# Cross-attention with text and prompt keys: when a Gram's rows are sent, and two moves in the first batch

## The chip, the cores and the metric

The kernel runs on one core of one Trainium2 chip. The metric is the device time of one execution in microseconds. The core has a matrix engine (TensorE; PE in the profile, with PEld for its weight loads), a vector engine (VectorE, DVE), an activation engine (ScalarE, ACT), a general engine (GpSimd, POOL), and SyncE (SP), which here issues nearly all DMAs. Each engine works through its own queue in order, and an instruction waits on semaphores for what it needs; whatever stands behind a waiting instruction on that engine waits too. An issue of a DMA takes time on SP's queue, and the data land later. Accumulators for matmuls lie in PSUM, in banks.

## The reference

Eight batches of 112 query rows with 320 channels attend, in 20 heads of 16 channels, to 375 context rows of 512 channels: 371 text rows and 4 prompt rows ("ip"). Besides the usual text attention, each head's attention-weighted mean of the raw context (`qsem`) is compared by cosine with the normalised prompt rows, and this similarity joins the prompts' logits.

```python
q, k_t, v_t = heads(hidden @ W_q), heads(text_ehs @ W_k), heads(text_ehs @ W_v)
probs_t = softmax(einsum("bhsd,bhtd->bhst", q, k_t) * Dh**-0.5)
text_out = einsum("bhst,bhtd->bhsd", probs_t, v_t)
k_ip, v_ip = heads(ip_ehs @ W_k_ip), heads(ip_ehs @ W_v_ip)
qsem = l2norm(einsum("bhst,bte->bhse", probs_t, text_ehs))
sem = einsum("bhse,bne->bhsn", qsem, l2norm(ip_ehs))
probs_ip = softmax(einsum("bhsd,bhnd->bhsn", q, k_ip) * Dh**-0.5 + 0.5 * sem)
ip_out = einsum("bhsn,bhnd->bhsd", probs_ip * spatial_mask, v_ip)
out = (text_out + ip_out) @ W_out + b_out + hidden
```

## The kernel before

The kernel never forms `qsem`. For each batch it makes the Gram matrix of the context rows (375 x 375, its upper triangle, `gram`, L516), beside it a column of ones and the values of one head. A head's probabilities, multiplied with this wide matrix `u`, give at once the product with the Gram (whose sum with the probabilities is the squared length of `qsem`), the products with the normalised prompts, the sum of the probabilities, and the text output. All in float32.

**Steps.** A step is a batch b and a group g of four heads, five groups to a batch, 40 steps. In a step TensorE does the big product of four heads (`multiplied`, L768, twelve blocks j = 0 to 11, each four matmuls, one for each head in its own 32 rows of the array and its own PSUM bank), and the scores of the step two ahead (`scores`, L709): the heads 2 and 3 at the step's start, the heads 0 and 1 at block j = 6. `probabilities` (L738) takes the maxima on DVE (`nmx`, L742), the exponentials on ACT (L745), and `sent` (L751) copies each head's probabilities by a DMA from SP into `xg` (L754), where the four heads lie as the transposition wants them. `xg` is a ring of two buffers: a step's buffer is that of the step two before. In the step before they are needed, at j = 2, DVE transposes them in blocks of 32 (`transposed`, L756, instruction L762) into `xgT`. After the product, ACT copies out the narrow columns (`value_sums`, L791) and DVE multiplies each bank with the probabilities and sums (`reduced`, L823, "junk"), which also frees the bank.

**Between products** TensorE computes the next batch's Gram (after g = 0), values (after g = 1 and 2) and keys (after g = 2, 3 and 4), projections of queries, and the rest of the batch before (`finish`, L844). The function `between` (L1112) writes this order out. `transposed_context` (L429) turns the context of a later batch for this, in three pieces on DVE (L437, for batches from 2 on); `run(("c", n), ...)` takes one piece.

**The wide matrix.** `doubled` (L502) writes the Gram into the tile `ug`, whose 128 partitions hold four blocks of 32 context rows. The product needs each block under every one of the four heads' 32 rows, so `gram_to_groups` (L549) copies each of four blocks (`QN`, numbered 0 to 3) four times (`parts`, one for each head's rows a) into `u`: sixteen DMAs from SP for a batch, 99 KB each (L553), each a whole row of `u` with the columns kept for the values. `u` has two buffers. The values go to DRAM (`values_to_dram`, L626) and come back by four DMAs as `vr` (`values_to_groups`, L632). Then `placed` (L681) copies, on GpSimd, the values of one group into the value columns of `u`, in three pieces (L688): for the next group of the same batch once the present product has read the old ones, and for g = 0 of the next batch at the end of step (b, 4), once all rows of its `u` and its `vr` have landed.

**What sets the order.** TensorE, SP, DVE and (in the main loop) ACT run the order in which the program issues; on GpSimd the framework chooses the order, except in the last batch. In the loop from L1246, a step issues the first pair's scores and probabilities, then the product with its insertions at j = 0, 2 and 6, then the second pair's probabilities, the sums, and behind them loads, `between` and the writing of the values. So SP sees in a step: the first pair's two sends; what is issued at j = 2; the second pair's two sends; what follows the second pair. The steps (6, 3) and (6, 4), ahead of the last batch, send three pairs instead of two: of those, the middle one (`more`) has its scores made at j = 0 and is sent at j = 2, ahead of the Gram's pieces there. In step (0, 3) (`late`) the first pair comes inside the product at j = 0. The last batch has a loop of its own (L1337).

In the first batch the prompts' projections are done by `prompt_projections` (L296), in pieces at the ends of (0, 1), (0, 2) and (0, 3); the second makes `kipb`, the prompts' keys under a mask, for `prompt_logits` (L690) at the end of (0, 4).

Of the kernel before, what the change touches and what calls it, by code (L numbers as in the profile page):

```python
# [20 lines left out]
def kernel(  # L21
# [14 lines left out]
    nc = tc.nc  # L36
# [259 lines left out]
    def prompt_projections():  # L296

        both = work.tile([2 * N, CP], F32, tag="ipkv", name="ipkv", bufs=1)
        kp = both[:N]
        last = kp[:, FULL * P :].rearrange("n (a r d) -> n a r d", r=2, d=D)  # L300
        nc.gpsimd.memset(last[:, :, 1, :], 0.0)
        ps = bank("ps_ipkv")
        for e in range(NE):
            for i, w in enumerate((wkip_sb, wvip_sb)):
                nc.tensor.matmul(
                    ps[i * N : (i + 1) * N, :C],
                    ipT[:, e, :],
                    w[:, e, :],
                    start=(e == 0),
                    stop=(e == NE - 1),  # L310
                )
        nc.scalar.copy(kp[:, : FULL * P], ps[:N, : FULL * P])
        nc.scalar.copy(
            last[:, :, 0, :], ps[:N, FULL * P : C].rearrange("n (a d) -> n a d", d=D)
        )
        nc.scalar.copy(both[N : 2 * N, :C], ps[N : 2 * N, :C])
        yield

        ps = bank("ps_kip")
        for i in range(NC):  # L320
            nc.tensor.transpose(
                ps[:, i * N : (i + 1) * N], kp[:, i * P : (i + 1) * P], ident[:N, :N]
            )
        nc.scalar.copy(kip, ps[:, : NC * N].rearrange("p (i n) -> p i n", n=N))
        for i in range(NC):
            nc.vector.tensor_tensor(
                kipb[:, i],
                kip[:, i, :NIP].unsqueeze(1).to_broadcast([P, HC, NIP]),
                hmask.unsqueeze(2).to_broadcast([P, HC, NIP]),
                ALU.mult,  # L330
            )
        yield

        nc.sync.dma_start(vipd, both[N : 2 * N, :C])
        yield
# [213 lines left out]
    def gram_to_groups(b, blocks, eng=nc.sync, parts=range(GROUP)):  # L549

        for q in blocks:
            for a in parts:
                eng.dma_start(  # L553
                    st[b]["u"][a * RG : (a + 1) * RG, q * GW : (q + 1) * GW],
                    ug[q * RG : (q + 1) * RG, :],
                )
# [181 lines left out]
    def probabilities(b, g, a, hold=False):  # L738
        s = st[b]
        ps = s.pop(("sc", g, a))  # L740
        nmx = small.tile([S, 1], F32, tag="nmx", name=f"nmx_{b}_{g}_{a}", bufs=4)
        nc.vector.tensor_reduce(nmx, ps[:S, :TT], AX.X, ALU.max, negate=True)  # L742
        if ("p", g) not in s:
            s["p", g] = home(b, g)
        nc.scalar.activation(s["p", g][:, a, :], ps[:S, :TT], AF.Exp, bias=nmx)  # L745
        if b > 0:
            nc.scalar.copy(s["ipl"][:, groups[g][a], :], ps[:S, TT:T])  # L747
        if not hold:
            sent(b, g, a)
# [355 lines left out]
    def run(key, make, pieces=1):  # L1105

        if key not in gens:
            gens[key] = make()
        for _ in range(pieces):
            next(gens[key], None)  # L1110

    def between(b, g):  # L1112

        nb = b + 1
        new = nb < B


        first = [bs for bs in pairs if bs[0] == (nb if b == 0 else nb + 1)]
        rest = [bs for bs in pairs if bs[0] == nb]
        if g == 0:  # L1120
            if new:
                run(("g", nb), lambda: gram(nb), 2)
            if new:
                run(("g", nb), None)
            if b == 0:
                run(("v", nb), None)
            if b > 0 and new:
                run(("f", b - 1), lambda: finish(b - 1))
        if g == 1:
            if new:  # L1130
                run(("v", nb), lambda: values(nb), 1 if b == 0 else 2)
            if b == 0:
                run(("pp",), prompt_projections)
        if g == 2 and new:
            run(("k", nb), lambda: keys(nb))
            run(("v", nb), None)
            for bs in first if b == 0 else ():
                run(("q", bs[0]), None)
        if g == 2 and b > 0 and new:
            run(("f", b - 1), None, 2)  # L1140
        if g == 3:
            if new:
                run(("k", nb), None, 1)
            if b > 0 and new:
                run(("f", b - 1), None)
            for bs in rest:
                run(("q", bs[0]), None)
        if nb + 1 < B and g in ((1, 2, 3) if b == 0 else (0, 1, 2)):
            run(("c", nb + 1), lambda: transposed_context(nb + 1))
        for bs in first:  # L1150
            if g in ((0, 1) if b == 0 else (2, 3)[: len(bs)]):
                run(("q", bs[0]), lambda: project_queries(bs))
        if g == 4:
            if b > 0 and new:
                run(("f", b - 1), None, 2)
            if nb < B - 1:
                run(("k", nb), None, 1)
            for bs in (first if b > 0 else []) + (rest if b < B - 2 else []):
                run(("q", bs[0]), None)
# [68 lines left out]
        (2, NG - 1): ((5, 0), (6, 1)),  # L1228
        (4, NG - 1): ((7, 0),),
    }  # L1230
    ctx_blocks = {1: (0,), 2: (1,), NG - 1: (2, 3)}
    halves = (range(GROUP // 2), range(GROUP // 2, GROUP))

    def ahead(n):

# [10 lines left out]
    for n, (b, g) in enumerate(steps[:-NG]):  # L1246
        now, more, then = ahead(n)
        late = (b, g) == (0, NG - 2)
        for c, a in now if not late else ():
            scores(*c, a)  # L1250
            probabilities(*c, a)
        for j, _ in enumerate(multiplied(b, g)):
            if j == 0:
                for c, a in now if late else ():
                    scores(*c, a)
                    probabilities(*c, a)
                for c, a in more:
                    scores(*c, a, ps=bank(f"ps_s_{c[0]}_{c[1]}_{a}"))
                    probabilities(*c, a, hold=True)
            if j == 6:  # L1260
                for c, a in then:
                    scores(*c, a)
            if j == 2:
                if g == 0:
                    gram_banks(b + 1)
                transposed(*steps[n + 1])
                for c, a in more:
                    sent(*c, a)
                if 1 <= g <= 3:
                    gram_to_groups(b + 1, {1: (0,), 2: (1,), 3: (3,)}[g], parts=halves[g == 2])  # L1270
                for c, i in x_loads.get((b, g), ())[: int(n > 0)]:
                    load_x_blocks(c, i)

                if g in (1, 2) and b > 0:
                    run(("f", b - 1), None)
        value_sums(b, g)
        if g == 2 and b > 0:
            run(("f", b - 1), None)
        if n == NG - 1:
            run(("t", b), lambda: prompt_logits(b))  # L1280
        for c, a in then:
            probabilities(*c, a)
        if n == len(steps) - NG - 1:
            sums = shared(b, g, GROUP // 2)
            next(sums)
            reduced(b, g, 2)
        else:
            reduced(b, g)
        placed(*steps[n + 1])
        if g == 0 and b > 1:  # L1290
            run(("f", b - 2), None)
        load_rest(n)
        if n == 0:
            load_next(2)
        if g in ctx_blocks and b < B - 3:
            load_ctx_blocks(b + 3, ctx_blocks[g])
        for c, i in x_loads.get((b, g), ())[1:]:
            load_x_blocks(c, i)
        if g == 1:
            gram_to_groups(b + 1, (0,), parts=halves[1])  # L1300
            gram_to_groups(b + 1, (1,), parts=halves[0])
        elif g == 2:
            gram_to_groups(b + 1, (2,))
        elif g == 3:
            gram_to_groups(b + 1, (3,), parts=halves[1])
            values_to_groups(b + 1)
        if g in (2, 3) and b == 0:
            run(("pp",), None)
        if (b, g) == (B - 2, 0):
            prompt_values_by_head()  # L1310
        if (b, g) == (B - 2, 1):
            bd = load_prompt_values_by_head()
        if g == 0 and b > 0:
            prompt_values(b - 1)
        between(b, g)
        if g == 1:
            values_to_dram(b + 1, nc.sync, 0, 2)
        if g == 2:
            values_to_dram(b + 1, nc.sync, 2)
# [137 lines left out]
```

## Time and profile before

| | us |
|---|---|
| median of 3 runs | 426.23 (425.27 to 430.86) |
| the profiled execution | 426.04 |
| its span in the profile | 424.3 |
| DMA: mean rate over the span | 155 GB/s |
| xg sends: count, each | 156, 162.3 KB |
| u pieces: count on SP, each | 124, 99.0 KB |

The profile was taken on one execution; its time of 426.04 us is the span of 424.3 and 1.7 us around it, and all positions below are microseconds from the start of the span. The granted clock was 0.999. A row of an engine's instructions in order of time has start, length, engine, line, operation, what is written and read, and their number; in brackets the idle time of the engine ahead of it and what ended it. A row of the busy time by stretches has the stretch, its length, then for PE, PEld, DVE, ACT and POOL the busy time with the number of instructions, the clock, and the DMA engines' share and rate.

### The profile page before, as it was taken

To read this page: it belongs to the slowest core of one execution; us is meant where nothing else is said; L and a number is where in the kernel's file an instruction comes from. 1 tells how busy PE (TensorE), PEld (TensorE's weight loads), DVE (VectorE), ACT (ScalarE), POOL (GpSimd) and SP (SyncE) were. 2 spreads that over 40 slices of the span, in tenths; PEclk is the share of its full clock that TensorE was granted. 3 is DMA by queue.
4 is the path that set the end of the run, shared out by engine and by line. 5 is a ranking of instruction groups with operands and counts; after the bars stand their busy time and mean duration, and the time that the engine had idled before them with its cause. 6 is when DMAs were issued, how large, how long until landed. Compare 5 with 4: busy or idle time off the path is not lost.

```text
span 424.3 us, 14021 instructions
## 1 busy us (share of the span) xinstructions
PE 415.8 (98%) x5500; PEld 327.3 (77%) x5500; DVE 331.5 (78%) x693; ACT 185.5 (44%) x647; POOL 111.2 (26%) x277
## 2 busy tenths in 40 slices
PE   8999999999998999999999999999999999999995
PEld 8867767878776977779778887788778887787993
DVE  5037668869896987889789987987898986888873
ACT  2344332335333463334533463333634363446773
POOL 6411100011160120602133220602124120515550
PEclk9999999999999999999999999999999999999999
DMA  8676846565766565666656556655555556465200
GB/s 256 184 191 198 187 122 181 155 174 152 192 157 169 141 170 154 158 175 175 169 142 167 144 158 164 159 145 158 167 151 151 134 162 181 135 167 166 66 2 29
DMA packets 61687, 65.84 MB, mean 155 GB/s; under 512 B 22072, under 2 KB 55648, under 8 KB 61622
## 3 DMA queue, kind: packets, MB, share of 16 engines
q1 hardware_dynamic: 60990, 63.98, 56.5%
q8 instruction: 44, 0.72, 0.8%
q10 hardware_dynamic: 632, 0.96, 0.7%
q14 instruction: 21, 0.17, 0.1%
HBM read 20.23 MB, written 5.32 MB: 60 GB/s over the span
## 4 chain that ended last, share of the span: by engine, by line
PE 83%; DVE 4%; ACT 3%; DMA 3%; issue 3%; SPq 2%; POOL 0%; DVEq 0%; POOLq 0%
PE ps_qd L781 34%; PE ps_v L611 14%; PE ps_k L577 10%; PE ps_s L719 9%; PE ps_g L535 7%; DMA xg<-p 2%; PE ps_q L377 2%; PE ps_o L995 2%; PE ps_g L491 1%; DVE xgT L762 1%; DVE nmx L742 1%; ACT shared L820 1%; SPq L553 1%; PE ps_w L467 1%; SPq L636 1%
## 5 line engine op out<-in xcount | busy, mean ns | idle before, releaser
L781 PE MATMUL ps_qd<-u,xgT 32*112 32x360 f32 (+11 forms) x3840 | 219.5, 351 | 1.2 <-POOL u L688 1.2
L781 PEld LDWEIGHTS ps_qd<-u,xgT 32*112 32x112 f32 x3840 | 189.1, 172 | 27.0 <-POOL u L688 2.4
L762 DVE STREAM_TRANSPOSE xgT<-xg 128x1536 f32<-128x1536 f32 (+1 forms) x45 | 119.7, 2680 | 13.9 <-DMA xg<-p 9.4
L745 ACT ACTIVATE p<-ps_s,nmx 112x371 f32<-112x371 f32 x156 | 84.9, 586 | 61.5 <-DVE nmx L742 49.3
L742 DVE TENSOR_REDUCE nmx<-ps_s 112x1 f32<-112x371 f32 x160 | 76.9, 526 | 28.3 <-PE ps_s L719 27.3
L827 DVE CUSTOM_DVE_ANT_0 junk<-ps_qd,p 112x371 f32<-112x371 f32 x146 | 79.2, 543 | 17.9 <-PE ps_qd L781 1.5
L719 PE MATMUL ps_s<-kT,qm 32*112 32x375 f32 (+1 forms) x320 | 66.7, 497 | 0.0
L688 POOL COPY u<-vr 128x64 f32<-128x64 f32 x120 | 25.7, 236 | 152.5 <-PE ps_qd L781 90.2
L611 PE MATMUL ps_v<-wv_sb,ctxT 128*128 128x384 f32 (+1 forms) x192 | 63.0, 477 | 0.0
L611 PEld LDWEIGHTS ps_v<-wv_sb,ctxT 128*128 128x128 f32 x192 | 35.7, 190 | 20.9
L794 ACT COPY pvs<-ps_qd 112x21 f32<-112x21 f32 x151 | 16.2, 189 | 74.8 <-PE ps_qd L781 74.5
L577 PE MATMUL ps_k<-ctxT,wk_sb 128*128 128x371 f32 x136 | 46.9, 488 | 0.2 <-DVE ctxT L458 0.2
L577 PEld LDWEIGHTS ps_k<-ctxT,wk_sb 128*128 128x128 f32 x136 | 24.4, 189 | 14.0 <-issue 0.5
L719 PEld LDWEIGHTS ps_s<-kT,qm 32*112 32x112 f32 x320 | 23.7, 170 | 12.6 <-issue 10.9
L535 PE MATMUL ps_g<-ctxT 128*32 128x375 f32 (+11 forms) x672 | 30.4, 333 | 0.0
L535 PEld LDWEIGHTS ps_g<-ctxT 128*32 128x32 f32 x672 | 27.7, 110 | 2.0
L618 ACT COPY vext<-ps_v 128x384 f32<-128x384 f32 (+1 forms) x24 | 11.2, 465 | 40.0 <-PE ps_v L611 39.5
L747 ACT COPY ipl<-ps_s 112x4 f32<-112x4 f32 x140 | 24.3, 174 | 0.0
L386 DVE TENSOR_SCALAR qm<-ps_q,emask 128x224 f32<-128x224 f32 (+1 forms) x25 | 9.0, 394 | 17.3 <-PE ps_q L377 17.2
L970 POOL TENSOR_TENSOR wv<-vip,w 112x1280 f32<-112x1280 f32 x6 | 14.8, 2464 | 27.7 <-DVE w L910 27.7
L437 DVE STREAM_TRANSPOSE ctxT<-ct 128x512 f32<-128x512 f32 x18 | 20.0, 1110 | 0.0
L508 POOL TENSOR_TENSOR ug<-ug,half 128x128 f32<-128x128 f32 (+1 forms) x24 | 10.4, 447 | 30.6 <-ACT ug L507 30.6
(174 smaller groups left out, 320.7 us busy)
## 6 DMA issues: line engine op xcount, KB each, us to landing
xg<-p SPq DMA_DIRECT2D x156, 162.3 KB
u<-ug SPq DMA_DIRECT2D x124, 99.0 KB
ct<-in_ctx_dram SPq DMA_DIRECT2D x24, 176.0 KB
vr<-vd SPq DMA_DIRECT2D x32, 120.0 KB
vip<-vipd SPq DMA_DIRECT2D x6, 560.0 KB
vd<-vext SPq DMA_DIRECT2D x7, 320.0 KB
vd<-vext SPq DMA_DIRECT2D x7, 160.0 KB
out_dram<-ob SPq DMA_DIRECT2D x8, 140.0 KB
```

Of the source, the lines that this page charges most:

```text
L437: nc.vector.transpose(ctxT[:, :, c * P : (c + 1) * P].rearrange("p e (j i) -> p j e i", i=RG), ct[:, some, :].rearrange("p j (k e) -> p j ...
L535: nc.tensor.matmul(ps[c][q * RG : (q + 1) * RG, j * RG - c * P : T - c * P], ctxT[:, e, j * RG : (j + 1) * RG], ctxT[:, e, j * RG : T], st ...
L577: nc.tensor.matmul(ps[:, :TT], wk_sb[:, e, i * P : (i + 1) * P], s["ctxT"][:, e, :TT], start=(e == 0), stop=(e == NE - 1),)
L611: nc.tensor.matmul(ps[:, :w], ctxT[:, e, c * P : (c + 1) * P], wv_sb[:, e, :w], start=(e == 0), stop=(e == NE - 1),)
L688: nc.gpsimd.tensor_copy(v, dealt(b, c, s["vr"][:, c * QN : (c + 1) * QN, g, :]))
L719: nc.tensor.matmul(ps[:S, :w], qm[a * RG : (a + 1) * RG, i, r, j * S : (j + 1) * S], s["kT"][a * RG : (a + 1) * RG, i, :w], start=True, st ...
L742: nc.vector.tensor_reduce(nmx, ps[:S, :TT], AX.X, ALU.max, negate=True)
L745: nc.scalar.activation(s["p", g][:, a, :], ps[:S, :TT], AF.Exp, bias=nmx)
L747: nc.scalar.copy(s["ipl"][:, groups[g][a], :], ps[:S, TT:T])
L762: nc.vector.transpose(xT[:, j : j + n].rearrange("p j (k q) -> p q j k", q=QN), xg[:, :, j * RG : (j + n) * RG].rearrange("p q (j k) -> p ...
L781: nc.tensor.matmul(banks[a][:S, j * RG : UW], xT[a * RG : (a + 1) * RG, j, :S], region(b, c)[a * RG : (a + 1) * RG, q, j * RG - c * P :], ...
L827: nc.vector.tensor_tensor_reduce(out=junk, in0=ps[:S, :TT], in1=s["p", g][:, a, :], scale=1.0, scalar=0.0, op0=ALU.mult, op1=ALU.add, accu ...
```

## The change

Three things are moved.

1. A Gram's sixteen pieces. Before: step (b, 1) sends half of block 0 at j = 2 and, after the second pair, the other half and half of block 1; (b, 2) sends the other half of block 1 at j = 2 and block 2 after the second pair; (b, 3) sends half of block 3 at j = 2 and the other half after the second pair, ahead of the values' four DMAs. After: the steps (b, 1) to (b, 4) send blocks 0 to 3, one whole block of four DMAs each, at j = 2; only the values' four DMAs stay behind the second pair of (b, 3).
2. The context's blocks. Before, step (b, 4) loads blocks 2 and 3 of context b + 3; after, only block 2, and block 3 is loaded at j = 2 of step (b + 1, 0).
3. First batch. `kipb`'s three products go from VectorE to GpSimd; the third piece of context 2's transposition goes from the end of (0, 3) to (0, 4), behind the first pair's probabilities.

```diff
-            nc.vector.tensor_tensor(
+            nc.gpsimd.tensor_tensor(
                 kipb[:, i],
...
-        if nb + 1 < B and g in ((1, 2, 3) if b == 0 else (0, 1, 2)):
+        if nb + 1 < B and g in ((1, 2) if b == 0 else (0, 1, 2)):
             run(("c", nb + 1), lambda: transposed_context(nb + 1))
...
-    ctx_blocks = {1: (0,), 2: (1,), NG - 1: (2, 3)}
-    halves = (range(GROUP // 2), range(GROUP // 2, GROUP))
+    ctx_blocks = {1: (0,), 2: (1,), NG - 1: (2,)}
...
             probabilities(*c, a)
+        if (b, g) == (0, NG - 1):
+            run(("c", LEAD), None)
         for j, _ in enumerate(multiplied(b, g)):
...
                 for c, a in more:
                     sent(*c, a)
-                if 1 <= g <= 3:
-                    gram_to_groups(b + 1, {1: (0,), 2: (1,), 3: (3,)}[g], parts=halves[g == 2])
+                if g > 0:
+                    gram_to_groups(b + 1, (g - 1,))
+                if g == 0 and 0 < b < B - 2:
+                    load_ctx_blocks(b + 2, (QN - 1,))
...
-        if g == 1:
-            gram_to_groups(b + 1, (0,), parts=halves[1])
-            gram_to_groups(b + 1, (1,), parts=halves[0])
-        elif g == 2:
-            gram_to_groups(b + 1, (2,))
-        elif g == 3:
-            gram_to_groups(b + 1, (3,), parts=halves[1])
+        if g == 3:
             values_to_groups(b + 1)
```

## The prediction

> **What bounds the kernel now.** I read the page first: busy time, then the chain of waits.
>
> ```profile
> PE 415.8 (98%) x5500; PEld 327.3 (77%) x5500; DVE 331.5 (78%) x693; ACT 185.5 (44%) x647; POOL 111.2 (26%) x277
> ...
> PE 83%; DVE 4%; ACT 3%; DMA 3%; issue 3%; SPq 2%; POOL 0%; DVEq 0%; POOLq 0%
> ```
>
> TensorE is busy almost throughout, so work taken off DVE, ACT, POOL or SP is worth only what TensorE now waits for. The busy time by stretches shows where it waits for nothing: batch 2's end to batch 3's start.
>
> ```profile
> 150.10:199.20 49.10, 49.10 (x686) 38.19 (x684) 41.60 (x83) 20.76 (x76) 12.36 (x29) 1.00 0.62 165
> ```
>
> No idle time in 49.10 us. The gaps are elsewhere; TensorE's instructions in order of time give three of them, two marked idle and one inside a step. (A step (b, g) is a batch and a group; it begins with the scores of L719.)
>
> ```profile
> 89.23 3.89 PE L781 MATMUL ps_qd<-u,xgT 32*112 32x392 f32 x54 [0.68 <-POOL u L688]
> ...
> 98.92 0.57 PE L719 MATMUL ps_s<-kT,qm 32*112 32x375 f32 x2
> ...
> 104.99 5.43 PE L611 MATMUL ps_v<-wv_sb,ctxT 128*128 128x384 f32 x16
> ...
> 137.88 0.54 PE L568 MATMUL ps_k<-ident,k 128*128 128x128 f32 x3 [1.33 <-ACT ipl L747]
> ```
>
> ```profile
> 180.05 0.57 PE L719 MATMUL ps_s<-kT,qm 32*112 32x375 f32 x2
> ...
> 188.68 0.57 PE L719 MATMUL ps_s<-kT,qm 32*112 32x375 f32 x2
> ...
> 194.04 4.34 PE L535 MATMUL ps_g<-ctxT 128*32 128x375 f32 x96
> ```
>
> A step's product takes 194.04 - 188.68 = 5.36 us when undisturbed; in (1, 1) it takes 104.99 - 98.92 = 6.07, so 0.7 is lost there. With 0.68 and 1.33 that makes 2.7 us that a better order could return. A gain of over 2% (8.5 us; 2% is about what a measurement of this kernel can tell from no change) has no room.
>
> **The new wait.** Block 3 of a Gram moves from step (b, 3) to (b, 4), behind that step's first pair. The copy at L688 (`placed`) writes value columns over those the rows just brought, so `placed(b + 1, 0)` must wait for all sixteen pieces, and TensorE's first product of batch b + 1 waits for it. What counts is when the last pieces land against that product's start. Prices, first in step (2, 4):
>
> ```profile
> 182.06 0.58 ACT L745 ACTIVATE p<-ps_s,nmx 112x371 f32<-112x371 f32 x1
> ...
> 186.29 0.62 ACT L745 ACTIVATE p<-ps_s,nmx 112x371 f32<-112x371 f32 x1
> ```
>
> ```profile
> 180.69 2.16 SPq L636 DMA_DIRECT2D vr<-vd  x4
> 182.95 1.85 SPq L754 DMA_DIRECT2D xg<-p  x2
> 184.85 1.88 SPq L127 DMA_DIRECT2D xr_sb<-in_x_dram  x4
> 186.83 1.74 SPq L754 DMA_DIRECT2D xg<-p  x2
> ...
> 207.57 2.51 SPq L553 DMA_DIRECT2D u<-ug  x4
> ```
>
> ```profile
> 185.52 0.59 POOL L688 COPY u<-vr 128x64 f32<-128x64 f32 x3 [8.22 <-DMA vr<-vd]
> ```
>
> The first pair's second exponential ends at 182.64. SP today sends the pair from 182.95, because the value rows (vr) keep it until 182.85; with two u pieces fewer ahead of them it is free earlier, the pair goes at about 182.1 and is out at 183.9 (today's start would make it 184.8). Four u pieces take 2.51: out at 186.4 (187.3). From the end of issuing to landing the trace has no row for u; the nearest is vr: 182.85 to 185.5 = 2.65 here, and 86.54 to 88.94 = 2.40 in the first batch (rows below). A u piece is smaller, so I take 2.4. Landed at 188.8, first of the three copies (0.59 / 3 = 0.2, with its waits 0.3) at 189.1, against a product due at 188.7: 0.4 to 0.5 late, 1.35 by today's start. I take 0.5 (0.4 to 1.35), and the same for (3, 4) and (4, 4), on the assumption that their steps have this length of 8.63. Step (5, 4) is shorter:
>
> ```profile
> 325.07 0.57 PE L719 MATMUL ps_s<-kT,qm 32*112 32x375 f32 x2
> ...
> 333.22 0.57 PE L719 MATMUL ps_s<-kT,qm 32*112 32x375 f32 x2
> ```
>
> 8.15 instead of 8.63, so 1.0 late (0.9 to 1.8). Together 3 x 0.5 + 1.0 = **+2.5** (2.1 to 5.9).
>
> [...]
>
> **The last hand-over, (6, 4) to (7, 0),** has another order. There the second pair's scores are made early and held, and its sends stand ahead of the Gram's pieces on SP.
>
> ```profile
> 372.82 0.58 PE L719 MATMUL ps_s<-kT,qm 32*112 32x375 f32 x2
> ...
> 380.93 1.29 PE L781 MATMUL ps_qd<-u,xgT 32*112 32x392 f32 x10 [0.26 <-POOL u L688]
> ```
>
> ```profile
> 375.55 2.98 DVE L762 STREAM_TRANSPOSE xgT<-xg 128x768 f32<-128x768 f32 x2
> ```
>
> ```profile
> 378.31 5.47 SPq L754 DMA_DIRECT2D xg<-p  x6
> ```
>
> The held pair is for (7, 2), whose ring buffer is the one that the transposition of (7, 0) reads; so it can't go before 375.55 + 2.98 = 378.5, however early SP is. Two sends at 5.47 / 6 = 0.91: 380.4. Four pieces, 2.5: 382.9. Landing 2.4: 385.3; copy 0.3: 385.6. The product started at 380.93: **+4.7** (4.3 to 5.0). Behind it TensorE, DVE and ACT work through the last batch in series, so I count it whole.
>
> **First batch.** Here SP runs without a gap:
>
> ```profile
> 79.09 1.83 SPq L754 DMA_DIRECT2D xg<-p  x2
> 80.97 0.52 SPq L1217 DMA_DIRECT2D sm_sb<-in_fside_S_dram  x1
> 81.56 0.40 SPq L1218 DMA_DIRECT2D bias_sb<-in_L_xattn_b_out_dram  x1
> 82.01 1.23 SPq L553 DMA_DIRECT2D u<-ug  x2
> 83.28 3.26 SPq L636 DMA_DIRECT2D vr<-vd  x4
> 86.58 0.47 SPq L334 DMA_DIRECT2D vipd<-ipkv  x1
> 87.15 3.66 SPq L754 DMA_DIRECT2D xg<-p  x4
> ```
>
> ```profile
> 77.09 0.58 ACT L745 ACTIVATE p<-ps_s,nmx 112x371 f32<-112x371 f32 x1
> ```
>
> ```profile
> 88.94 0.58 POOL L688 COPY u<-vr 128x64 f32<-128x64 f32 x3 [7.07 <-DMA vipd<-ipkv]
> ```
>
> Steps (0, 1) and (0, 2) lose two pieces each behind their second pair, so SP reaches (0, 3)'s second pair when its exponentials end (77.7) and not at 79.09. From there: pair 1.8, two constants 1.0, vr 3.3 (2.2 if it issues as at 180.69), vipd 0.5, first pair of (0, 4) 1.8, four pieces 2.5: out at 88.6 (87.5), landed 91.0 (89.9), copy done 91.3 (90.2) against 89.23. One thing delays it: (0, 1) has SP busy too, and two more pieces ahead of its second pair push the transposition of (0, 3) by 1.2, so the upper bound is 91.6. **+1.8** (1.0 to 2.4). TensorE being later, the 0.7 in (1, 1) is recovered: **-0.7**.
>
> **First batch on DVE.** The prompts' keys and the context's transposition:
>
> ```profile
> 69.36 0.39 DVE L326 TENSOR_TENSOR kipb<-kip,hmask 128x32 f32<-128x32 f32 x3
> ...
> 80.18 1.09 DVE L437 STREAM_TRANSPOSE ctxT<-ct 128x512 f32<-128x512 f32 x1
> ```
>
> ```profile
> L508 POOL TENSOR_TENSOR ug<-ug,half 128x128 f32<-128x128 f32 (+1 forms) x24 | 10.4, 447 | 30.6 <-ACT ug L507 30.6
> ```
>
> DVE gets 0.39 back; on POOL three products of 32 columns cost at most 3 x 0.45 = 1.3, needed only for the logits at the end of (0, 4), in an engine that is busy 26%: nothing. The transposition (1.09) no longer stands ahead of (0, 4)'s first maxima, so its exponentials end a microsecond earlier. Both gains shorten (0, 3) and (0, 4), and the wait ahead of (1, 0), which is set by SP, is late next: I count nothing beside the +1.8. The context's last block, two DMAs moved from (b, 4) to (b + 1, 0), is needed some 9 us later at L437; hidden, and if late DVE waits first.
>
> **The gap at 137.88.** It comes from a second pair sent late in (1, 3), since SP was still on the first:
>
> ```profile
> 121.10 3.68 SPq L553 DMA_DIRECT2D u<-ug  x4
> 124.88 0.54 SPq L627 DMA_DIRECT2D vd<-vext  x1
> 125.53 1.86 SPq L754 DMA_DIRECT2D xg<-p  x2
> ```
>
> ```profile
> 123.25 0.58 ACT L745 ACTIVATE p<-ps_s,nmx 112x371 f32<-112x371 f32 x1
> ```
>
> The pair was ready at 123.8, half of it earlier; SP, without the four u pieces at 121.10, sends it about 2 us sooner, which pays for two more pieces (1.25) behind it. The gap of 1.33 goes; what is late next is the wait for u, about 0.25 in this longer step: **-1.1**. In the other steps pairs are ready some 4 us apart (182.64 and 186.9 above), and a pair (1.85) with four pieces (2.5) fills that: nothing gained or lost.
>
> **Sum:** 1.8 - 0.7 - 1.1 + 2.5 + 4.7 = +7.2. The profiled execution took 426.04 us (span 424.3 and 1.7 around it), 0.2 under the median of 426.23: 433.2, or 1.6% more. With every term at its bound: 1.0 - 0.7 - 1.1 + 2.1 + 4.3 = +5.6 to 2.4 + 0 + 0 + 5.9 + 5.0 = +13.3, so 431.6 to 439.3.
>
> **Rivals.** *The rows are in time* (not slower). If pieces land sooner than vr does and the last batch's order takes up its delay (its end waits for exponentials and sums in series, so some slack may hide there), the waits at the heads of batches vanish and the 2.7 us are returned: 423.3; with one of the two half true, up to 426. For it: TensorE's wait at 89.23 is only 0.68 with SP saturated. Against: the ring buffer at 378.5 is a fixed point. It decides from 186.4 + 2.0, a landing within 2.0 us. 0.2.
>
> [...] 0.15.
>
> *Late pairs* (slower by over 2%). In (2, 4) and (4, 4) four loads of x (L127, 184.85) follow the pieces and stand ahead of the second pair, which today leaves at 186.83 as its exponentials end; 2.5 us later it delays the next transposition, and sums, and the release of TensorE's banks. If half of that reaches TensorE in both, and SP's start in (b, 4) is today's: the upper end, 437 to 439. For it: DVE is busy 41.60 of 49.10. Against: these loads stand there today without an idle moment. 0.2.
>
> *My forecast:* 0.45, of which a fifth lies over 2%. So slower by over 2% (434.8): 0.2 + 0.09 = 0.29; faster 0.02; within 0.69. The range leaves out half of the first rival and the end of the third: 424.5 to 437.5.
>
> **What would show it.** In the new profile TensorE's first L781 of batches 3 to 7 shows idle time with POOL u L688 as releaser, about 0.5, 1.0 at batch 6 and 4.7 at batch 7; POOL's idle time there ends by DMA u; the gap before L568 in (1, 4) is gone; L326 is on POOL. No such waits, and I am wrong on the landing; waits but a time as before, and the tail had slack.

## The result, and the profile after

The changed kernel takes 441.77 us (median of 6 runs, 439.7 to 445.22) beside 425.75 for the kernel before (6 runs: the three of the table above and three more). The ratio is 1.0402, 95% interval 1.0358 to 1.0445; it is 441.77 over 424.70, the median of those three more. The kernel is slower, by more than twice what was forecast (433.2), and outside the range (up to 437.5). The profiled execution took 440.86 us, with a span of 439.1: 14.8 more than the 424.3 of before.

The page of the changed kernel: busy time, the clock in 40 slices, the chain of waits.

```profile
PE 422.1 (96%) x5500; PEld 333.3 (76%) x5500; DVE 331.3 (75%) x690; ACT 185.4 (42%) x647; POOL 111.7 (25%) x280
...
PEclk9999999989999999999999999999999999998999
...
PE 81%; SPq 6%; DVE 3%; ACT 3%; DMA 3%; issue 2%; POOL 1%; POOLq 0%; DVEq 0%
```

SP's queue grew from 2% to 6% of the chain, about 26 us beside 8. TensorE is also 6.3 us *busier* (422.1 against 415.8) with the same 5500 instructions, and the clock has a dent in slice 9 and one in slice 37. The first view of waits (who <- whom: us, times, longest), the changed kernel's and then the one of before:

```profile
POOL u L688 <- DMA u<-ug: 44.7, 5, 11.8
...
PEld ps_qd L781 <- POOL u L688: 13.3, 7, 5.8
PE ps_qd L781 <- POOL u L688: 9.5, 6, 5.3
```

```profile
PEld ps_qd L781 <- POOL u L688: 2.4, 3, 1.3
PE ps_qd L781 <- POOL u L688: 1.2, 3, 0.7
```

GpSimd's copy now waits for the Gram's pieces, and TensorE for that copy, as forecast. But 9.5 - 1.2 = 8.3 us of waiting isn't 14.8. TensorE's instructions in order of time show the first reason:

```profile
89.24 3.38 PE L781 MATMUL ps_qd<-u,xgT 32*112 32x392 f32 x23 [2.22 <-POOL u L688]
...
239.13 0.89 PE L719 MATMUL ps_s<-kT,qm 32*112 32x375 f32 x4
...
240.74 1.71 PE L781 MATMUL ps_qd<-u,xgT 32*112 32x392 f32 x15 [0.72 <-POOL u L688]
...
394.25 2.32 PE L781 MATMUL ps_qd<-u,xgT 32*112 32x392 f32 x10 [5.26 <-POOL u L688]
```

The wait of 0.72 at 240.74 is short only in the row. The step began at 239.13 with its four scores' matmuls; before, such a step starts its product 0.02 us after the first scores and runs the two side by side. So this product is 240.74 - 239.13 - 0.02 = 1.6 late. What a step loses has to be taken from the starts of its first product, not from idle time. By that measure, from TensorE's rows in both traces (us; step lengths are from first product to first product):

| from - to | before | after | lost | forecast |
|---|---|---|---|---|
| start of (1, 0) | 89.23 | 89.24 | 0.0 | +1.8 |
| (1, 0) - (1, 1) | 9.70 | 11.40 | +1.7 | 0 |
| (1, 1) - (1, 2) | 11.43 | 10.72 | -0.7 | -0.7 |
| (1, 2) - (2, 0) | 29.15 | 28.91 | -0.2 | -1.1 |
| (2, 4) - (3, 0) | 8.63 | 9.61 | +1.0 | +0.5 |
| (3, 1) - (3, 2) | 10.72 | 11.42 | +0.7 | 0 |
| (3, 4) - (4, 0) | 8.63 | 10.23 | +1.6 | +0.5 |
| (4, 4) - (5, 0) | 8.62 | 8.65 | 0.0 | +0.5 |
| (5, 0) - (5, 2) | 20.36 | 22.04 | +1.7 | 0 |
| (5, 4) - (6, 0) | 8.20 | 10.37 | +2.2 | +1.0 |
| (6, 3) - (6, 4) | 9.75 | 10.16 | +0.4 | 0 |
| (6, 4) - (7, 0) | 7.98 | 12.98 | +5.0 | +4.7 |
| (7, 0) - (7, 1) | 9.01 | 10.42 | +1.4 | 0 |
| sum | | | 14.8 | 7.2 |

Two of the unforeseen losses, in (1, 0) and (7, 0), come right behind the two longest waits. The busy time by stretches, with the granted clock behind POOL's column:

```profile
90.26:93.67 3.41, 3.41 (x32) 3.41 (x28) 2.34 (x1) 0.00 (x0) 0.86 (x1) 0.50 0.73 202
93.67:94.00 0.33, 0.33 (x12) 0.33 (x10) 0.33 (x1) 0.00 (x0) 0.04 (x1) 1.00 0.75 230
393.70:394.04 0.34, 0.00 (x0) 0.00 (x0) 0.00 (x0) 0.00 (x0) 0.08 (x1) 1.00 0.53 118
394.04:397.45 3.41, 3.20 (x21) 3.16 (x25) 0.07 (x1) 0.00 (x0) 0.50 (x3) 0.50 0.61 175
```

Twice TensorE ran at half clock for 3.41 us. Half of 3.41 is 1.7, the loss in (1, 0); half of the 3.20 busy at (7, 0) is 1.6, beside a loss of 1.4. It is busy time, and so in no row of waits: some 3.3 of the 6.3 us that TensorE is busier. A product that is held up inside its step shows as busy too; (5, 0) and (5, 1) lose 1.7 us with TensorE busy for all of their 22.04.

SP's queue around the hand-overs to batches 4 and 7:

```profile
229.29 1.84 SPq L754 DMA_DIRECT2D xg<-p  x2
231.18 2.08 SPq L636 DMA_DIRECT2D vr<-vd  x4
233.37 1.74 SPq L754 DMA_DIRECT2D xg<-p  x2
235.16 3.37 SPq L553 DMA_DIRECT2D u<-ug  x4
...
382.53 3.44 SPq L636 DMA_DIRECT2D vr<-vd  x4
...
386.08 3.57 SPq L754 DMA_DIRECT2D xg<-p  x4
389.70 2.49 SPq L553 DMA_DIRECT2D u<-ug  x4
```

From 229.29 on SP has no gap: the second pair of (3, 3), the value rows, the first pair of (3, 4), the pieces. The pair leaves at 233.37, 2.86 us after the step's product began at 230.51 (2.05 was forecast), and the four pieces take 3.37 instead of 2.5. GpSimd's first copies in those places:

```profile
190.13 0.59 POOL L688 COPY u<-vr 128x64 f32<-128x64 f32 x3 [12.06 <-DMA xr_sb<-in_x_dram]
...
240.45 0.59 POOL L688 COPY u<-vr 128x64 f32<-128x64 f32 x3 [11.53 <-DMA u<-ug]
...
393.96 0.58 POOL L688 COPY u<-vr 128x64 f32<-128x64 f32 x3 [2.94 <-DMA u<-ug]
```

From the end of issuing to the copy: 240.45 - 238.53 = 1.92, and 393.96 - 392.19 = 1.77. So the pieces land sooner than the 2.4 of my row, only they leave later.

### The profile page after: what moved, and what is told of

Read it like the earlier page. It is cut to its first block, busy times and chain, and to the rows that moved or that the text cites. A ratio compares the mean times of both kernels' runs of the same rounds, so it can differ in the third digit from the quotient of the medians.

```text
span 439.1 us, 14016 instructions
## 1 busy us (share of the span) xinstructions
PE 422.1 (96%) x5500; PEld 333.3 (76%) x5500; DVE 331.3 (75%) x690; ACT 185.4 (42%) x647; POOL 111.7 (25%) x280
## 4 chain that ended last, share of the span: by engine, by line
PE 81%; SPq 6%; DVE 3%; ACT 3%; DMA 3%; issue 2%; POOL 1%; POOLq 0%; DVEq 0%
PE ps_qd L781 36%; PE ps_v L611 14%; PE ps_k L577 10%; PE ps_s L719 8%; PE ps_g L535 7%; SPq L553 3%; DMA u<-ug 2%; PE ps_q L377 2%; SPq L754 2%; SPq L636 1%; PE ps_g L491 1%; DMA ip_sb<-in_ctx_dram 1%; ACT shared L820 1%; DVE junk L827 1%; PE ps_k L593 1%
## 5 line engine op out<-in xcount | busy, mean ns | idle before, releaser
L781 PE MATMUL ps_qd<-u,xgT 32*112 32x360 f32 (+11 forms) x3840 | 223.5, 355 | 9.6 <-POOL u L688 9.5
L781 PEld LDWEIGHTS ps_qd<-u,xgT 32*112 32x112 f32 x3840 | 194.8, 173 | 36.0 <-POOL u L688 13.3
L719 PE MATMUL ps_s<-kT,qm 32*112 32x375 f32 (+1 forms) x320 | 67.7, 501 | 0.0
L719 PEld LDWEIGHTS ps_s<-kT,qm 32*112 32x112 f32 x320 | 24.7, 172 | 12.2 <-issue 10.2
L970 POOL TENSOR_TENSOR wv<-vip,w 112x1280 f32<-112x1280 f32 x6 | 14.8, 2468 | 28.7 <-DVE w L910 28.7
```

The source lines that it names most:

```text
L719: nc.tensor.matmul(ps[:S, :w], qm[a * RG : (a + 1) * RG, i, r, j * S : (j + 1) * S], s["kT"][a * RG : (a + 1) * RG, i, :w], start=True, st ...
L781: nc.tensor.matmul(banks[a][:S, j * RG : UW], xT[a * RG : (a + 1) * RG, j, :S], region(b, c)[a * RG : (a + 1) * RG, q, j * RG - c * P :], ...
```

## The experiments

The ratios are to the kernel before on the same chip, with 95% intervals.

**Which part costs.** `grams_alone` has only the first of the three moves, `small_moves_alone` only the other two. Against the changed kernel, the first of them:

```diff
-            nc.gpsimd.tensor_tensor(
+            nc.vector.tensor_tensor(
                 kipb[:, i],
...
-        if nb + 1 < B and g in ((1, 2) if b == 0 else (0, 1, 2)):
+        if nb + 1 < B and g in ((1, 2, 3) if b == 0 else (0, 1, 2)):
...
-        if (b, g) == (0, NG - 1):
-            run(("c", LEAD), None)
...
-    ctx_blocks = {1: (0,), 2: (1,), NG - 1: (2,)}
+    ctx_blocks = {1: (0,), 2: (1,), NG - 1: (2, 3)}
...
-                if g == 0 and 0 < b < B - 2:
-                    load_ctx_blocks(b + 2, (QN - 1,))
```

> The kernel before with the first part of the change alone (four whole blocks at j = 2 of groups 1 to 4). Theory A (the loss is made where a batch hands over to the next, by block 3 landing too late for the placed values): 438 to 444 us, the first product of batch 7 again some 13 us later than before the change. Rival B (a good part comes from the two small moves, the prompts' keys on GpSimd and the context's loads and turn): at least 4 us less than the changed kernel, under 437.

Measured: 439.95 us, ratio 1.0355 (1.0293 to 1.0417), over the rival's 437. Batch 7's first product comes at 392.62, 11.7 later than before (13.3 in the changed kernel).

The other takes the hunk of `gram_to_groups` back instead:

```diff
-                if g > 0:
-                    gram_to_groups(b + 1, (g - 1,))
+                if 1 <= g <= 3:
+                    gram_to_groups(b + 1, {1: (0,), 2: (1,), 3: (3,)}[g], parts=halves[g == 2])
...
-        if g == 3:
+        if g == 1:
+            gram_to_groups(b + 1, (0,), parts=halves[1])
+            gram_to_groups(b + 1, (1,), parts=halves[0])
+        elif g == 2:
+            gram_to_groups(b + 1, (2,))
+        elif g == 3:
+            gram_to_groups(b + 1, (3,), parts=halves[1])
             values_to_groups(b + 1)
```

> The kernel before with the other two parts alone (context block 3 loaded a group later; prompts' keys on GpSimd; the context's third turn in (0, 4)). Theory A: 424.5 to 427 us, within 0.5% of before, since TensorE waits in the first batch on SP and not on VectorE. Rival B: 429 us or more.

Measured: 425.25 us, ratio 1.0016 (0.9976 to 1.0056). In the total the Gram's pieces cost nearly everything, and the two small moves are not measurable. In the steps of its profile they are: the product of (1, 0) starts at 87.33 instead of 89.23, and (5, 0) and (5, 1) together take 21.70 instead of 20.36.

**All sixteen pieces by group 3**, still whole blocks:

```diff
-                if g > 0:
-                    gram_to_groups(b + 1, (g - 1,))
+                if 1 <= g <= 3:
+                    gram_to_groups(b + 1, ((0, 1, 3)[g - 1],))
...
+        if g == 2:
+            gram_to_groups(b + 1, (2,))
         if g == 3:
             values_to_groups(b + 1)
```

> The changed kernel, but all sixteen pieces are sent by group 3: blocks 0, 1 and 3 whole behind the first pair of groups 1, 2 and 3, block 2 behind the second pair of group 2. Theory A: no first product of a batch waits for the rows, 422 to 427 us. Rival C (four pieces between a group's two pairs delay the second pairs, and that is what costs): three of the four blocks still stand there, so 434 us or more.

Measured: 430.53 us, ratio 1.0123 (1.0049 to 1.0197), between the two expectations. TensorE's rows:

```profile
140.57 0.54 PE L568 MATMUL ps_k<-ident,k 128*128 128x128 f32 x3 [1.91 <-ACT ipl L747]
...
240.19 0.54 PE L568 MATMUL ps_k<-ident,k 128*128 128x128 f32 x3 [0.71 <-ACT ipl L747]
...
338.50 0.54 PE L568 MATMUL ps_k<-ident,k 128*128 128x128 f32 x3 [0.94 <-ACT ipl L747]
```

The waits for rows at batches 2 to 6 are gone; gaps at L568, the kind that was 1.33 at 137.88 before, stand in their place. The first products of batches 1 and 7 still wait, 1.30 and 0.80. By the ratios a late block is about two thirds of the loss. That whole blocks ahead of a second pair are the rest was not tested by itself.

**The half clock.** Products of identities into a spare bank, which nothing reads, fill the two long waits of the changed kernel:

```diff
         if (b, g) == (0, NG - 1):
             run(("c", LEAD), None)
+        if (b, g) == (1, 0):
+            awake(7, end=True)
...
+        if g == 0:
+            awake(18, end=True)
         for j, _ in enumerate(multiplied(b, g)):
             if g == 0 and j in (0, 3):
```

> The changed kernel with matmuls of an identity on itself put in front of the first products of batch 1 (7 of them) and batch 7 (18), while those wait; they add work that nothing reads. Theory D (TensorE runs at half its clock for 3.4 us after these two waits because it stood idle): clock 1.0 throughout, from the first product of batch 1 to that of (1, 1) 9.7 us instead of 11.4, and 3 us less in all, 438 to 439.5 us. Rival E (the matmuls there are slow for another reason, such as the DMAs that land at the same time): 441 us or more, and the product of (1, 0) is as slow as before.

Measured: 438.73 us, ratio 1.0329 (1.0263 to 1.0395). Its stretches behind the first products of (1, 0) and (7, 0):

```profile
91.40:95.00 3.60, 3.60 (x55) 3.60 (x59) 1.48 (x1) 0.14 (x1) 1.30 (x4) 1.00 0.71 198
392.70:396.00 3.30, 3.30 (x46) 3.29 (x49) 1.59 (x3) 1.01 (x4) 0.23 (x2) 1.00 0.43 126
```

Full clock in both: (1, 0) is back to 9.70 (its product starts at 91.39, that of (1, 1) at 101.09) and (7, 0) to 9.01 (392.64 and 401.65). That is 3.1 less in the two steps, and the total is 3.0 under 441.77; the intervals of the two ratios overlap, so it is the steps that show it. The waits themselves remain.

**Block 3 without SP's queue:** ScalarE issues that block.

```diff
-                    gram_to_groups(b + 1, (g - 1,))
+                    gram_to_groups(b + 1, (g - 1,), nc.scalar if g == NG - 1 else nc.sync)
```

> The changed kernel with block 3's four pieces issued by ScalarE at the same place of the program, so that SP has only a pair, the loads and a pair in group 4. Theory A with F (the rows are late because SP is late with them, not because they fly long: in the changed kernel they land 1.7 to 1.9 us after the last issue): they are out about 5 us after a step's start, none of the batches 1 to 7 waits for them, and with the first batch's gain of the small moves the time is 421 to 425 us, at or under the kernel before. Rival G (four pieces ahead of the second pair in groups 1 to 3 still cost, as blocks sent by group 3 did, or ScalarE's own work is pushed back by 2.4 us of issuing): 428 us or more.

Measured: 428.90 us, ratio 1.0085 (1.0042 to 1.0127). TensorE's rows with a wait of over 0.5 at the hand-overs:

```profile
89.90 5.36 PE L781 MATMUL ps_qd<-u,xgT 32*112 32x392 f32 x56 [2.42 <-POOL u L688]
...
334.18 0.54 PE L568 MATMUL ps_k<-ident,k 128*128 128x128 f32 x3 [0.76 <-ACT ipl L747]
...
383.87 1.29 PE L781 MATMUL ps_qd<-u,xgT 32*112 32x392 f32 x10 [0.79 <-POOL u L688]
```

At batch 7 the 5.26 became 0.79, and at batches 2 to 6 no idle time for rows is over 0.3. So the place on SP's queue made most of batch 7's wait. But 421 to 425 us was missed and the rival's 428 or more came, and by the measure of the table (3, 4) still takes 9.26 and (5, 4) 9.49 (8.63 and 8.20 before). Issues of ScalarE and of SP, and GpSimd's copy, at the hand-over to batch 4:

```profile
230.44 0.51 ACTq L553 DMA_DIRECT2D u<-ug  x1
231.00 1.90 ACTq L553 DMA_DIRECT2D u<-ug  x3
```

```profile
232.29 5.02 SPq L754 DMA_DIRECT2D xg<-p  x4
```

```profile
237.41 0.59 POOL L688 COPY u<-vr 128x64 f32<-128x64 f32 x3 [10.56 <-DMA xg<-p]
```

The pieces are issued by 232.90, 4.5 us after the step's product began, 3.6 earlier than in the changed kernel. The copy comes 4.5 after that instead of 1.9. Its row names a send as the releaser, but the semaphore of the last piece is complete only at 237.30 in the trace, 4.4 after the issue; in the changed kernel that took 1.6. At the hand-over to batch 1 it took 5.5 (issued by 83.31, landed at 88.83), and there the wait stayed, 2.42, with a half clock behind it. So beside SP's sends, which took 5.02 for four instead of 3.58, the pieces do fly long, and the theory that only their place in the queue makes them late is half right.

**Block 3 on SP, but ahead of the first pair of (b, 4):**

```diff
         late = (b, g) == (0, NG - 2)
+        if g == NG - 1:
+            gram_to_groups(b + 1, (g - 1,))
...
-                if g > 0:
+                if 0 < g < NG - 1:
                     gram_to_groups(b + 1, (g - 1,))
```

> The changed kernel with block 3's pieces issued by SP at the start of group 4, ahead of that group's first pair. Theory A with F: SP is usually idle there, so the rows land in time at batches 1 to 6 and about 1.3 us late at batch 7; the pairs go later by up to 1.5 us. 425 to 430 us. Rival G: the later pairs cost as much as the rows did, 435 us or more.

Measured: 430.98 us, ratio 1.0134 (1.0075 to 1.0193); span 425.8; 1 us over what was expected, and 4 under the rival. The profiled execution (428.30) is the fastest of its four, the others took 430.95 to 431.24. In it TensorE waits 0.89 at batch 1 and 0.66 at batch 7 for rows, and under 0.3 between. These are the same pieces from the same queue, issued 1.2 to 2.6 us earlier in the step, 4.6 at batch 7. In their place (2, 1), (3, 1) and (5, 1) each take some 1.0 longer than before.

**The loads of x** that stood between the pieces and the second pair, put behind that pair:

```diff
-                for c, i in x_loads.get((b, g), ())[: int(n > 0)]:
+                for c, i in x_loads.get((b, g), ())[: int(n > 0 and g == 0)]:
                     load_x_blocks(c, i)
...
-        for c, i in x_loads.get((b, g), ())[1:]:
+        for c, i in x_loads.get((b, g), ())[int(g == 0) :]:
```

> The changed kernel with the loads of x in (2, 4) and (4, 4) moved behind the second pair. Theory H (of the loss, 2.4 us in (3, 1), (5, 0) and (5, 1) come from second pairs that leave late behind the pieces and these loads): 438 to 440.5 us, and those steps as long as before the change. Rival: 441 us or more, the steps as long as in the changed kernel.

Measured: 438.77 us, ratio 1.0346 (1.0276 to 1.0415). The step (3, 1) takes 10.72 again (from 200.25 to 210.97) instead of 11.42 (200.12 to 211.54); (5, 0) and (5, 1) take 20.35 instead of 22.04. Together 2.4. The totals show less: the intervals of this ratio and of 1.0402 overlap, and this profile has no half clock at batch 1.

**The last hand-over:** the pieces ahead of the held pair's sends.

```diff
-                for c, a in more:
-                    sent(*c, a)
                 if g > 0:
                     gram_to_groups(b + 1, (g - 1,))
+                for c, a in more:
+                    sent(*c, a)
```

> The changed kernel with the pieces ahead of the held pair in (6, 3) and (6, 4). If the held pair is what makes batch 7 wait, the rows leave SP 1.8 us earlier and batch 7's first product waits 3.2 to 3.5 us instead of 5.3; the time falls by 1.5 to 2, to 439.5 to 441. If SP was busy anyway and the pair only fills its time, less than 0.5 is gained.

Measured: 439.14 us, ratio 1.0332 (1.0264 to 1.0400). TensorE's row:

```profile
393.97 2.32 PE L781 MATMUL ps_qd<-u,xgT 32*112 32x392 f32 x10 [3.51 <-POOL u L688]
```

5.26 became 3.51: the 1.8 us of two sends. The total came out just under the 439.5 to 441 expected. The half clock stayed; both its stretches were twice as long in this profile (89.16 to 95.98 and 392.94 to 399.77), and its clock over the whole span was 0.982 beside 0.991 in the changed kernel.

**The value rows off SP's queue.** ScalarE issues them, so nothing but pairs stands ahead of the pieces in (b, 4).

```diff
-    def values_to_groups(b):
+    def values_to_groups(b, eng=nc.sync):
...
-            nc.sync.dma_start(
+            eng.dma_start(
                 s["vr"]
...
-            values_to_groups(b + 1)
+            values_to_groups(b + 1, nc.scalar)
```

> The changed kernel with the four DMAs of the value rows issued by ScalarE. Theory (SyncE's queue is full from the second pair of (b, 3) to the last piece in (b, 4), because the value rows, 2.1 us, stand ahead of the first pair of (b, 4); that is why the pieces left late): the waits for the rows at the first products of batches 4 and 6 fall from 1.6 and 2.2 us to under 0.5, batch 7 keeps its 5.0, the total is 437 to 440. Rival (the pieces are late by their landing, or the value rows now land late behind ScalarE's exponentials and set the same wait): waits of 1 us or more stay at batches 4 and 6, total 440 to 444.

Measured: 438.58 us, ratio 1.0309 (1.0240 to 1.0378). SP's rows and then TensorE's:

```profile
231.09 4.53 SPq L754 DMA_DIRECT2D xg<-p  x4
235.68 3.40 SPq L553 DMA_DIRECT2D u<-ug  x4
```

```profile
240.07 0.54 PE L568 MATMUL ps_k<-ident,k 128*128 128x128 f32 x3 [1.01 <-ACT ipl L747]
...
394.27 2.32 PE L781 MATMUL ps_qd<-u,xgT 32*112 32x392 f32 x10 [4.34 <-POOL u L688]
```

The number came as expected, batch 7 kept 4.34, and the waits for rows at batches 4 and 6 are gone, but much of them returned as gaps at L568 (1.01 here): (3, 4) to (4, 0) lasts 9.85, against 10.23 in the changed kernel and 8.63 before, and (5, 4) to (6, 0) 9.36, against 10.37 and 8.20. And SP hardly got freer: its four sends took 4.53 instead of 1.84 + 1.74, the pieces 3.40 as before. The theory is half right: taking issues off SP moves the transfers, it doesn't thin them out.

**Two cures together,** block 3 ahead of the first pair and the loads of x behind the second (the two edits above):

> The changed kernel with two cures at once: block 3 goes ahead of the first pair in step (b, 4), and the loads of x in group 4 go behind the second pair. Theory (each cause of the loss has its own price, and they add): the run with the first cure alone stood at a ratio of 1.0134 with a span of 425.8; its steps after batches 2 and 4 still held late second pairs, so the second cure returns up to 1 us at (3, 1) and (5, 1): span 423.5 to 425.5, ratio 1.000 to 1.012, no wait for rows over 1 us. Rival (block 3 ahead of the first pair delays the whole chain of pairs, whatever stands behind it): span 425.5 to 428, ratio at or above that of the first cure alone.

Measured: 428.69 us, ratio 1.0086 (1.0055 to 1.0117), span 428.0. The ratio lies in what the theory allowed and under that of the first cure alone; the span lies at the rival's upper end. The 425.8 that the expected spans were reckoned from was the shortest of that run's four (425.8 to 429.3). (3, 1) to (3, 2) takes 10.83 instead of 11.67 with the first cure alone, and (5, 1) to (5, 2) 10.72 instead of 11.75, which is what the second cure should return. This profile has another gap instead:

```profile
138.09 0.54 PE L568 MATMUL ps_k<-ident,k 128*128 128x128 f32 x3 [1.41 <-ACT ipl L747]
```

The intervals of the two runs overlap, so whether the totals add isn't settled. No version beats the kernel before; the four in which block 3 is earlier or comes from ScalarE lie at ratios of 1.0085 to 1.0134.

## Why the prediction was wrong, point by point

The direction and the mechanism held: the pieces of block 3 land late, `placed` waits for them, TensorE for `placed`, most of all at the last hand-over. What failed is the sum, which put two terms at nothing and mis-sized others. The 14.8 - 7.2 = 7.6 us are +3.1 for the clock, +2.4 for late pairs, +2.3 for the hand-overs to batches 3 to 6, -0.9 for the first batch and the gap, +0.3 for the last hand-over, and +0.4 in (6, 3), whose cause is open. Without the first two terms even the sum with every term at its bound, 439.3, stays below what was measured, and the range stated ended lower still, at 437.5.

**A term was missing: the clock behind a wait, +3.1** (1.7 at (1, 0), 1.4 at (7, 0)). I priced a wait at its length. The run with identity products shows that the two longest cost 3 us more. The trace of before could not show it: the longest of its three gaps was 1.33, with the clock at 0.999. In the changed kernel both stretches of half clock last 3.41 us; which waits had one behind them in the other runs stands in the last section.

**The late pairs behind the loads of x, +2.4,** were a rival at 0.2 and should have been in the sum. My reason against, that these loads stand there today without an idle moment, compares different queues: in the kernel before the second pair leaves as its exponentials end, with nothing to spare, so 2.5 us of pieces ahead of it were likely to show. DVE's transposition of the pairs shows it (the changed kernel in step (5, 0), then the same step of before):

```profile
295.24 3.17 DVE L762 STREAM_TRANSPOSE xgT<-xg 128x1536 f32<-128x1536 f32 x1 [3.42 <-DMA xg<-p]
```

```profile
289.39 3.05 DVE L762 STREAM_TRANSPOSE xgT<-xg 128x1536 f32<-128x1536 f32 x1 [1.74 <-DMA xg<-p]
```

It starts 5.3 us after the step's product instead of 3.6 (289.94 and 285.75). The steps (5, 0) and (5, 1) lose 1.7 together, and the run with the loads moved gives it back. But the pieces are not needed for it. With the small moves alone no piece is moved, and yet the first pair of (4, 4) leaves 4.15 after the step's product instead of 3.33, the transposition starts 5.0 after that of (5, 0) (287.49 and 282.50), and the two steps lose 1.3. With the pieces alone, on the other hand, (3, 1) takes its old 10.72. What is shown is that a pair behind these loads has no room; what pushes it differs from run to run.

**Hand-overs to batches 3 to 6: 4.8 instead of 2.5,** inside the bounds of 2.1 to 5.9, but wrong by parts. The failed step is "with two u pieces fewer ahead of them it is free earlier, the pair goes at about 182.1". In (2, 4) and (4, 4) it held within 0.3 us. In (3, 4) and (5, 4) the pair goes 2.9 and 3.4 after the product's start. I had looked at the length of the steps (b, 4) and not at those of (b, 3): (3, 3) takes 8.34 before, (2, 3) 9.49, so in the shorter one SP's work no longer fits, and the value rows push the pair. The second slip there is the price of the pieces: 2.51 is their price where little else moves. Stretches of the changed kernel from the first pair's start to the issue behind the last piece, for the hand-overs to batches 3, 4, 5 and 6 (the two last columns: share of the DMA engines, GB/s):

```profile
182.89:187.22 4.33, 4.33 (x86) 3.92 (x81) 4.08 (x6) 1.51 (x10) 0.00 (x0) 1.00 0.65 153
233.37:238.63 5.26, 5.26 (x83) 4.49 (x76) 4.85 (x8) 2.03 (x9) 0.00 (x0) 1.00 0.82 170
283.62:287.94 4.32, 4.32 (x83) 3.82 (x77) 4.10 (x6) 1.50 (x9) 0.00 (x0) 1.00 0.64 158
334.32:339.39 5.07, 4.51 (x74) 3.51 (x67) 4.51 (x6) 1.64 (x9) 0.00 (x0) 1.00 0.89 176
```

The pieces took 2.49 with the DMA engines 0.65 and 0.64 busy, and 3.37 and 3.17 with 0.82 and 0.89. That the busy engines hold up SP's issue is read from this and from the two runs with issues on ScalarE; it was not tested by itself.

Against these, the **landing** was over-priced: 1.92, 1.75, 1.76 and 1.77 at batches 4, 5, 6 and 7 where I took 2.4 from the value rows; only at batch 3 it was longer, 190.13 - 187.18 = 2.95. GpSimd's row there names the loads of x behind the pieces, but it was the last piece: fifteen of the sixteen updates of its semaphore had come by 188.74 and the last at 190.08. The quick landing hid the slip at batch 5 (0.0 late). A landing within 2.0 us, from which the first rival was to be decided, came at these four; at batches 4, 6 and 7 the rows were late all the same, because the pieces left SP later than I had them.

**The first batch: 0.0 instead of +1.8, and the gap: -0.2 instead of -1.1.** My working slipped here: the copy done at 91.3 is 2.1 after 89.23, and 1.8 is the landing at 91.0. In the profile the product of (1, 0) came at 89.24. SP was ahead of my list: the second pair left at 76.85 instead of 77.7, and the value rows took 1.96 instead of 3.3, so the pieces were out at 87.03 instead of 88.6, and the copy came 1.92 later. But five profiles with SP's order unchanged up to there have it at 89.24, 89.78, 90.77, 90.81 and 91.39 (the last behind the added products), and the run with the small moves alone at 87.33 where before has 89.23: a spread of 2 us, in which the forecast lies. This term is not decided by one profile. The -0.7 came as forecast, but it doesn't hang on TensorE being later: with the small moves alone (1, 0) starts 1.9 earlier than before and (1, 1) takes the same 10.72. The gap at 137.88 did go; the wait for u behind it is 1.1 and not 0.25 (28.91 against 29.15 - 1.33 = 27.82), the same lateness as at batch 3.

**The last hand-over, +4.7, measured +5.0,** held with its order: transposition (ends 386.84), held pair, pieces, landing, copy. The pieces start 2.86 after the transposition's end rather than 1.8, since the value rows, 3.44 long, had pushed the first pair too; the short landing gave most of that back.

With the rows earlier nothing was won either (1.0085 to 1.0134 in four versions), so the 2.7 us that a better order could return never showed.

## What to carry to other kernels

Price an idle time of TensorE at its length plus the half clock that can follow it (here 3.41 us, which cost 1.7 and 1.4), and look for the dent in the clock's row before adding up waits. Where a transfer is moved to a later step, write out the whole queue of its issuer through the shortest pair of steps, with the durations of a stretch where the DMA engines are as busy (four pieces took 2.49 us here with them 0.65 busy, and 3.37 with 0.82), and see what leaves last, the moved transfer or the one it now stands ahead of. Where it is moved to another queue, its landing has to be priced anew: 4.4 and 5.5 us here instead of 1.6. Measure a step's loss from its first product to the next one, because work that runs side by side otherwise hides a wait (0.72 in its row here, 1.6 in the step).

## What the runs showed of the hardware

The clock fell to 0.50 behind waits of 5.26 and 2.22 us in the changed kernel, 2.42 with the block on ScalarE, 1.67 with the value rows on ScalarE, 1.91 and 1.30 with all blocks by group 3. It stayed at 1.00 behind 2.05 with the loads of x moved, and behind 1.41 with two cures, 1.33 in the kernel before, 1.28 behind the identity products, 1.01 with the value rows on ScalarE, and 0.89 with block 3 ahead of the first pair. So the length of a wait doesn't tell by itself: 1.30 and 1.67 were enough in two runs, and 2.05 was not in another. The 3.41 us ahead of the first drop, and those ahead of the second, in the changed kernel; then the same of the run with all blocks by group 3; then a stretch as long with the loads of x moved, behind which the clock stayed:

```profile
86.85:90.26 3.41, 1.19 (x13) 1.02 (x15) 1.82 (x5) 1.55 (x6) 0.58 (x3) 1.00 0.60 149
390.63:394.04 3.41, 0.00 (x0) 0.00 (x0) 0.00 (x0) 0.00 (x0) 0.47 (x2) 1.00 0.67 164
```

```profile
86.77:90.18 3.41, 2.46 (x10) 1.24 (x8) 2.98 (x12) 1.51 (x5) 0.00 (x0) 1.00 0.63 159
137.97:141.38 3.41, 1.50 (x9) 0.98 (x8) 3.27 (x6) 1.38 (x5) 0.59 (x3) 1.00 0.35 98
```

```profile
86.58:89.99 3.41, 2.13 (x10) 1.24 (x10) 2.98 (x12) 1.28 (x5) 0.00 (x0) 1.00 0.68 161
```

TensorE was still busy for 1.19, 2.46 and 1.50 us of the 3.41 ahead of three of the drops, and kept its clock behind a stretch with 2.13. In the changed kernel the stretch from 387.22 to 390.63, with 1.77 busy, was followed by full clock. So no limit on the busy share of these stretches fits all of them, and what the chip counts stays open.

The return is clearer. Ahead of the kernel's end the half clock lasted 3.41 us wherever TensorE was busy for 2.96 us or more of them, and twice as long in the four places where it was busy for less of the first 3.41: 1.76 and 2.38 with the pieces ahead of the held pair, 2.11 with the pieces alone, 1.65 with the value rows on ScalarE. At (7, 0) that made the step 11.35 to 11.71 long instead of 10.42.
